# One input plane of a fused four-layer convolution: from a VectorE subtraction to a ScalarE copy and an accumulating transfer

## The chip, the cores and the metric

The kernel runs on one core of one Trainium2 chip. The metric is device time in microseconds of the whole program, as a median of several runs. Engines are named as the profile names them: PE is TensorE's matmul, PEld its weight load, DVE is VectorE, ACT is ScalarE, POOL is GpSimd, SP is SyncE, which issues most transfers.

## The reference

A batch of 128 signals with 64 channels and 1024 positions goes through four convolution layers with 3 taps each. Every layer's weights are scaled per sample by a style vector and normalised. The third layer keeps the length, the second doubles it and blurs, the fourth blurs and halves it. The input is added at the end. Cut to what matters:

```
for i, typ in enumerate(('same', 'upsample', 'same', 'downsample')):
    s = style @ mod_w[i].T + mod_b[i]
    weight = SCALE * w[i] * s[:, None, :, None]
    weight = weight * rsqrt(sum(weight * weight, axis=(2, 3)) + EPS)[:, :, None, None]
    out = conv(out, weight) + b[i]        # with a blur in 'upsample' and 'downsample'
return x + out
```

## The kernel before

No nonlinearity stands between the layers, so the kernel composes the four convolutions of each sample into one set of 9 taps (three groups of three) and applies that set to the input. The work goes in 32 quads of four samples. For one quad the taps are made in stages (scale3, stage1, stage2, stage3, combine), each a group of small matmuls on PE and a scaled copy out of PSUM on ACT. The taps are then applied by a fast-convolution scheme with five products, conv0 to conv4. Each product is a group of 24 matmul instructions over 340 columns, and each has an input tile of its own, made from the planes of X:

- X is the quad's input in SBUF, as three interleaved planes per sample pair. There are two X buffers, and SP reloads one while the other is in use.
- `T3` is plane 3 minus plane 1 and is the input of conv3. It has two buffers.
- `T12` holds the inputs of conv1 (in1) and conv2 (in2), and `T04` those of conv0 and conv4. They come from G, a combination of X planes that DVE makes (in_g01 and in_g2).

The loop is software-pipelined. Turn q computes the products of quads q and n = q+1, the taps of quad c = q+2 and the start of the chain of quad q+4. A turn's order is written out by hand in `turn_of(q)`; each engine runs its instructions in the order in which this function issues them, and semaphores do the rest. On PE a turn of the steady part is: stage2(c), conv2(q), stage3_b(c), conv4(q), stage3_a(c), conv3(n), stage1_a, conv0(q), stage1_b and share, conv1(n). On POOL it is r_sums(c) (L588), in2(n) (L731), a small sum of the S tile (L445), in1(c) (L726). On ACT stage2's copies to R are followed by the four small copies to psW that stage3_b asks for. On DVE `in3(c)` (L711) stands near the end of the turn, between sum1(n) (the tile y, L662) and the next turn's sum2 (the tile Y, L662).

Early turns (0 to 3), an entry turn (4) and the last three quads have orders of their own.

Of the kernel before, what the change touches and what calls it, by code (L numbers as in the profile page):

```python
# [49 lines left out]
AF = mybir.ActivationFunctionType  # L50
ALU = mybir.AluOpType
# [12 lines left out]
def kernel(  # L64
# [18 lines left out]
    nc_v, nc_a, nc_g = nc.vector, nc.scalar, nc.gpsimd  # L83
# [53 lines left out]
    NX = 2  # L137
    PL = NXC // 3
    Xs = [const.tile([P, 2, NXC], F32, name=f"X{i}") for i in range(NX)]

    def load(q, planes=slice(0, 3)):

        if q < NQ:
            at = slice(planes.start * PL, planes.stop * PL)
            for c in range(2):
                nc.sync.dma_start(Xs[q % NX][:, c, at], x[2 * q + c, :, at])
# [374 lines left out]
    def stage2(q, pool=None, engs=(nc_a, nc_a), between=None):  # L521
        st = chain[q]
        shared = q in shared_ps
        ps = stage2_rest(q) if shared else unit(pool or ps_w, f"psR{q}")
        for n, e in enumerate(() if shared else (-2, -1, 0, 1, 2, 3, 4, 5, 6)):
            if e % 2 == 0:
                a, lo, m = slice(1, 4), e // 2 + 1, 3
            else:
                a, lo, m = slice(4, 6), (e + 3) // 2, 2
            for r, rows in enumerate(HALF):  # L530
                for c, cols in enumerate(HALF):
                    src = st[c if r == 0 else 1 - c]
                    nc.tensor.matmul(  # L533
                        ps[r][cols, lo * C : (lo + m) * C],
                        E[rows, e + 2, :],
                        src[rows, a, :],
                        start=(n == 0),
                        stop=(n == 8),
                        skip_group_check=True,
                    )  # L540
        if between:
            between()
        t = r_pool.tile([P, 2, 9, C], F32, tag="R", name=f"R{q}")
        for r in range(2):
            scaled_copy(engs[r], flat(t[:, r, :7]), ps[r][:, : 7 * C], tC[:, q, r : r + 1])
        chain[q] = t
        return ps
# [38 lines left out]
    def r_sums(q, eng):  # L586
        t = chain[q]
        eng.tensor_add(t[:, :, 7:9], t[:, :, 2:6:3], t[:, :, 3:7:3])  # L588
# [72 lines left out]
    def sum_of(out, x, f, y, op=ALU.add):  # L661
        nc_v.scalar_tensor_tensor(out, x, f, y, op0=ALU.mult, op1=op)  # L662
# [6 lines left out]
    def combine_a(q):  # L669

        chain.pop(q)
        a, b, c, h1, h2, h3 = taps(q)
        sum_of(h1, c, -2.0, a)
        residual(q)
        sum_of(h3, h1, 1.0 / 6.0, b)

    def combine_b(q, steps=range(3)):

        a, b, c, h1, h2, h3 = taps(q)
        plan = (h2, c, -0.5, a), (h1, b, -3.0, h2, ALU.subtract), (h2, h2, -1.0 / 3.0, b)  # L680
        for i in steps:
            sum_of(*plan[i])


    NJ = NB + 2
# [7 lines left out]
    def plane(buf, i, pairs=BOTH_PAIRS):  # L693

        at = PL * (2 - i) if i < 3 else PL * 2 + 1
        return buf[:, pairs, at : at + NJ]

    def t_tile(q, tag):
        if (q, tag) not in Ts:
            Ts[q, tag] = tpool.tile([P, 2, 1 + (tag != "T3"), PL], F32, tag=tag, name=f"{tag}_{q}")  # L700
        return Ts[q, tag]

    def g_tile(q):
        if q not in Gs:
            Gs[q] = gpool.tile([P, 2, 3 * PL], F32, tag="G", name=f"G{q}")
        return Xs[q % NX], Gs[q]

    def in3(q, pairs=BOTH_PAIRS):
        if q < NQ:
            X, t = Xs[q % NX], t_tile(q, "T3")  # L710
            nc_v.tensor_sub(t[:, pairs, 0, :NJ], plane(X, 3, pairs), plane(X, 1, pairs))  # L711

    def in_g01(q, pairs=BOTH_PAIRS):
        if q < NQ:
            X, g = g_tile(q)
            sum_of(g[:, pairs, PL:], X[:, pairs, : 2 * PL], 0.5, X[:, pairs, PL:], ALU.subtract)
# [11 lines left out]
    def in2(q, eng):  # L728
        if q < NQ:
            t, g = t_tile(q, "T12"), Gs[q]  # L730
            eng.tensor_sub(t[:, :, 1, :NJ], plane(g, 2), plane(g, 1))  # L731
# [10 lines left out]
    def product(q, m, ps, groups=range(K)):  # L742

        W, H_ = Wq[q]
        tag, i = SLOT[m]
        for g in groups:
            for s, rows in enumerate(HALF):
                for c, cols in enumerate(HALF):
                    if m in (0, 4):
                        w = W[rows, tap(m // 2, g), c, :]  # L750
                    else:
                        w = H_[rows, m - 1, g, c, :]
                    nc.tensor.matmul(  # L753
                        ps[s][cols, :NB],
                        w,
                        Ts[q, tag][rows, c, i, g : g + NB],
                        start=(g == 0 and m == 3),
                        stop=(g == K - 1),
                        skip_group_check=True,
                    )  # L760
# [12 lines left out]
    def banks(q):  # L773
        return A[q] if isinstance(A[q], list) else [A[q][:, s] for s in range(2)]
# [3 lines left out]
    def open_a(q):  # L778
        A[q] = ps_conv.tile([P, 2, 512], F32, tag="u", name=f"psA{q}")
        return banks(q)  # L780

    def conv3(q, pool=None):
        if pool:
            A[q] = unit(pool, f"psA{q}")
        elif q not in A:
            open_a(q)
        product(q, 3, banks(q))
# [15 lines left out]
    def conv2(q, *groups):  # L803
        product(q, 2, banks(q), groups or range(K))

    def sum2(q, steps=(0, 1)):
        if 0 in steps:
            m3 = m3c.pop(q)
            for s, a in enumerate(banks(q)):
                sum_of(Y[:, s, :NB], m3[:, s], 3.0, a[:, :NB])  # L810
        for s, a in parts(q) if 1 in steps else ():
            nc_v.tensor_sub(y1w[q][:, s], y1w[q][:, s], a)  # L812

    def conv4(q, *groups):
        product(q, 4, Y_banks, groups or range(K))

    def conv0(q, *groups):
        product(q, 0, banks(q), groups)
# [403 lines left out]
    def high(n):  # L1222
        return Y[:, 1, NB + 4 : NB + 4 + n]
# [77 lines left out]
    def side(work, q):  # L1301
        work.get(q, lambda: None)()

    AHEAD = 3
    FIRST = AHEAD + 1

    def sharing(q):
        return FIRST < q < NQ - 4

# [104 lines left out]
    def turn_of(q):  # L1414
        n, c, s = q + 1, q + 2, q + 4
        entry = q == FIRST
        stage2(c)
        if entry:
            sum2(q)
            conv4(q)  # L1420
            combine_a(n)
            r_sums(c, nc_v)
        else:
            conv2(q)
            r_sums(c, nc_g)
            sum2(q)
            in2(n, nc_g)
        side(TABLES, q)
        for i in range(3):
            load(c + 1, slice(i, i + 1))  # L1430
        stage3_b(c, open_a(n))
        if entry:
            conv0(q, 0, 1)
        else:
            combine_a(n)
            conv4(q)
        stage3_a(c)
        combine_b(n)
        conv3(n)
        if entry:  # L1440
            copy_m3(n)
        outputs(q, 2)
        if s < NQ:
            stage1_a(s)
        if not entry:
            copy_m3(n)
        in04(n)
        if sharing(q):
            share_sums(c + 1)
        in_g2(c)  # L1450
        side(SIDE, q)
        if q in SMALL:
            l, bs = SMALL[q]
            nc_v.memset(high(bs.stop - bs.start), 0.0)
        conv0(q, *((2,) if entry else range(K)))
        if entry:
            conv1(n, 0, 1)
        outputs(q, 1)
        if s < NQ:
            stage1_b(s)  # L1460
        in_g01(c)
        if sharing(q):
            share(c + 1, banks(q))
            share_copy(c + 1)
        outputs(q, 0)
        if q in SLOTS:
            matmuls, width, rest = SLOTS[q]
            slot(matmuls, width, Y_banks)
            rest()
        if s == NQ:  # L1470
            slot(ends3, 3, unit(ps_w, "psE"), 3)
            rest3()
        if q in SMALL:
            small(q)
        conv1(n, *((2,) if entry else range(K)))
        sum1(n)
        in3(c)
        side(LATE, q)
        if s == NQ:
            in04(c)  # L1480
        in1(c, nc_g)
        if s + 1 < NQ:
            scale3(s + 1)

    for q in range(FIRST):
        early_turn(q)
    for q in range(FIRST, NQ - 3):
        turn_of(q)

    q, n, c = NQ - 3, NQ - 2, NQ - 1  # L1490
# [32 lines left out]
    q, n = NQ - 2, NQ - 1  # L1523
# [22 lines left out]
    q = NQ - 1  # L1546
# [90 lines left out]
```

## Time and profile before

| what | value |
|---|---|
| median of 3 runs | 480.38 us (480.28 to 481.21) |
| profiled execution, first to last instruction (span) | 478.0 us |
| PE busy in the span | 469.6 us |
| DVE busy | 417.5 us |
| ACT busy | 310.1 us |
| POOL busy | 163.5 us |
| bytes moved by the DMA engines | 70.70 MB |
| mean granted clock of TensorE | 0.997 |

No separate time of the profiled execution is given beside its span; the median of the runs is 2.4 us above the span, and that difference is what lies around the first and the last instruction. In a trace's list, "idle before" is how long the engine had nothing to do ahead of an instruction, and the arrow names what ended that idle time. "issue" is idle time for which the profile shows no wait at all.

### The profile page before, as it was taken

To read this page: it belongs to the slowest core of one execution; us is meant where nothing else is said; L and a number is where in the kernel's file an instruction comes from. 1 tells how busy PE (TensorE), PEld (TensorE's weight loads), DVE (VectorE), ACT (ScalarE), POOL (GpSimd) and SP (SyncE) were. 2 spreads that over 40 slices of the span, in tenths; PEclk is the share of its full clock that TensorE was granted. 3 is DMA by queue.
4 is the path that set the end of the run, shared out by engine and by line. 5 is a ranking of instruction groups with operands and counts; after the bars stand their busy time and mean duration, and the time that the engine had idled before them with its cause. 6 is when DMAs were issued, how large, how long until landed. Compare 5 with 4: busy or idle time off the path is not lost.

```text
span 478.0 us, 26721 instructions
## 1 busy us (share of the span) xinstructions
PE 469.6 (98%) x11928; PEld 346.4 (72%) x11928; DVE 417.5 (87%) x690; ACT 310.1 (65%) x708; POOL 163.5 (34%) x197
## 2 busy tenths in 40 slices
PE   8999999999999999999999999999999999999995
PEld 7877788777878876677776677766887777766652
DVE  5889998879889998899979899979989999999895
ACT  5565666667666676666667666667666768766352
POOL 3434032663335342243432233422434432333200
PEclk9999999999999999999999999999999999999998
DMA  5406365544445554345543455533455554445125
GB/s 175 158 28 200 114 195 192 150 139 144 139 150 157 173 173 127 122 151 160 171 149 120 131 170 152 173 127 126 145 169 162 162 154 146 152 146 170 61 91 191
DMA packets 50514, 70.70 MB, mean 148 GB/s; under 512 B 5664, under 2 KB 47328, under 8 KB 50400
## 3 DMA queue, kind: packets, MB, share of 16 engines
q1 hardware_dynamic: 49808, 68.32, 45.8%
q8 instruction: 93, 1.52, 1.5%
q10 hardware_dynamic: 592, 0.69, 0.5%
q14 instruction: 21, 0.17, 0.1%
HBM read 35.36 MB, written 33.62 MB: 144 GB/s over the span
## 4 chain that ended last, share of the span: by engine, by line
PE 95%; DVE 4%; issue 0%; ACT 0%; ACTq 0%; DVEq 0%
PE psA L753 45%; PE Y L753 11%; PE psR L467 9%; PE psA L571 7%; PE psW L571 7%; PE psS L389 6%; PE psR L533 4%; PE psA L467 2%; PE Y L994 2%; DVE H L662 1%; PE Y L180 1%; PE Y L336 1%; DVE G L662 0%; PE psM L204 0%; DVE o L832 0%
## 5 line engine op out<-in xcount | busy, mean ns | idle before, releaser
L753 PE MATMUL psA<-T,H 64*64 64x340 f32 x2304 | 187.3, 447 | 0.8 <-DVE y L662 0.7
L753 PEld LDWEIGHTS psA<-T,H 64*64 64x64 f32 x2304 | 89.9, 133 | 50.0 <-issue 3.1
L662 DVE SCALAR_TENSOR_TENSOR G<-X 128x1376 f32<-128x1376 f32 (+2 forms) x65 | 78.1, 1207 | 1.1 <-DMA X<-in_x 0.9
L726 POOL TENSOR_TENSOR T<-G 128x684 f32<-128x684 f32 x28 | 46.5, 1659 | 73.1 <-DVE G L662 73.1
L445 POOL TENSOR_TENSOR S<-S 128x128 f32<-128x128 f32 x28 | 22.1, 790 | 144.1 <-ACT S L360 136.8
L360 ACT ACTIVATE R<-psR,tC 128x448 f32<-128x448 f32 x63 | 36.5, 630 | 46.3 <-PE psR L467 26.7
L753 PE MATMUL psA<-T,Wf 64*64 64x340 f32 x768 | 63.9, 446 | 0.0
L753 PE MATMUL Y<-T,Wf 64*64 64x340 f32 x768 | 62.8, 451 | 0.1
L662 DVE SCALAR_TENSOR_TENSOR Y<-m,psA 128x340 f32<-128x340 f32 x64 | 33.1, 517 | 28.0 <-PE psA L753 26.6
L360 ACT ACTIVATE psW<-psA 128x128 f32<-128x128 f32 x100 | 19.3, 269 | 50.3 <-PE psA L571 46.2
L740 DVE TENSOR_TENSOR T<-G 128x1368 f32<-128x1368 f32 (+1 forms) x33 | 50.7, 1540 | 0.0
L360 ACT ACTIVATE Wf<-psW,t 128x256 f32<-128x256 f32 (+2 forms) x76 | 32.7, 479 | 26.5 <-PE psW L571 26.2
L711 DVE TENSOR_TENSOR T<-X 128x684 f32<-128x684 f32 x32 | 47.9, 1496 | 0.0
L467 PE MATMUL psR<-S,E 64*64 64x64 f32 (+1 forms) x1472 | 46.5, 238 | 0.0
L731 POOL TENSOR_TENSOR T<-G 128x684 f32<-128x684 f32 x28 | 46.5, 1660 | 0.0
L389 PEld LDWEIGHTS psS<-wd,w2n 64*64 64x64 f32 x1120 | 35.0, 133 | 13.3 <-ACT S L360 0.8
L467 PEld LDWEIGHTS psR<-S,E 64*64 64x64 f32 x1472 | 39.6, 134 | 5.2 <-ACT psR L490 0.2
L753 PEld LDWEIGHTS Y<-T,Wf 64*64 64x64 f32 x768 | 29.6, 132 | 18.0 <-DVE Y L662 0.7
L830 ACT ACTIVATE o<-psA,tb,td 128x340 f32<-128x340 f32 x63 | 37.0, 647 | 6.3 <-PE psA L753 6.3
L753 PEld LDWEIGHTS psA<-T,Wf 64*64 64x64 f32 x768 | 29.1, 133 | 15.1
L830 ACT ACTIVATE o<-Y,tb,td 128x340 f32<-128x340 f32 x63 | 36.6, 637 | 4.5 <-PE Y L753 2.7
L830 ACT ACTIVATE o<-y,tb,td 128x340 f32<-128x340 f32 x62 | 38.5, 679 | 0.6 <-DVE y L812 0.6
(165 smaller groups left out, 832.4 us busy)
## 6 DMA issues: line engine op xcount, KB each, us to landing
out<-o SPq DMA_DIRECT2D x167, 170.0 KB, 2.6
X<-in_x SPq DMA_DIRECT2D x150, 172.0 KB, 3.6
X<-in_x SPq DMA_DIRECT2D x14, 516.0 KB, 5.3
out<-o SPq DMA_DIRECT2D x6, 510.0 KB, 5.4
out<-o SPq DMA_DIRECT2D x2, 340.0 KB, 3.0
Xe<-in_x_ends SPq DMA_DIRECT2D x1, 512.0 KB, 6.7
out<-o ACTq DMA_DIRECT2D x3, 170.0 KB, 2.3
par<-in_params SPq DMA_DIRECT2D x2, 192.0 KB, 3.4
```

Of the source, the lines that this page charges most:

```text
L360: nc_a.activation(dst, src, AF.Copy, scale=f)
L389: nc.tensor.matmul(ps[r][cols, at * C : (at + n) * C], weight[rows], wd[c if r == 0 else 1 - c][rows, taps], start=first, stop=last, skip_ ...
L445: nc_g.tensor_add(t[:, :, 2], t[:, :, 2], t[:, :, 0])
L467: nc.tensor.matmul(dst[r][cols], weight[rows], st[c if r == 0 else 1 - c][rows, slots, :], start=False, stop=last, skip_group_check=True,)
L571: nc.tensor.matmul(dst[r][cols], weight[rows], t[rows, c, slots, :], start=first, stop=last, skip_group_check=True,)
L662: nc_v.scalar_tensor_tensor(out, x, f, y, op0=ALU.mult, op1=op)
L711: nc_v.tensor_sub(t[:, pairs, 0, :NJ], plane(X, 3, pairs), plane(X, 1, pairs))
L726: eng.tensor_add(t[:, :, 0, :NJ], plane(g, 2), plane(g, 1))
L731: eng.tensor_sub(t[:, :, 1, :NJ], plane(g, 2), plane(g, 1))
L740: nc_v.tensor_sub(t[:, pairs, :, :NJ], both(a, PL), both(b, 1))
L753: nc.tensor.matmul(ps[s][cols, :NB], w, Ts[q, tag][rows, c, i, g : g + NB], start=(g == 0 and m == 3), stop=(g == K - 1), skip_group_check ...
L830: nc_a.activation(dst, src, AF.Identity, bias=add, scale=d3)
```

## The change

For the quads 8 to 30 (the turns 6 to 28), T3 is made in another way. ACT writes minus plane 1 into the tile, right behind stage2's copies. A transfer that POOL issues behind in2(n) then reads plane 3 from DRAM and adds it to what stands in the tile. DVE's subtraction is dropped for these quads; for the others it stays.

```
+    def in3_negated(q):
+        X, t = Xs[q % NX], t_tile(q, "T3")
+        nc_a.activation(t[:, :, 0, :NJ], plane(X, 1), AF.Copy, scale=-1.0)
+
+    def in3_added(q):
+        t = t_tile(q, "T3")
+        at = PL * 2 + 1
+        nc_g.dma_start(
+            out=t[:, :, 0, :NJ],
+            in_=x[2 * q : 2 * q + 2, :, at : at + NJ].rearrange("b p j -> p b j"),
+            accum_op=ALU.add,
+        )
...
+    SUMMED = FIRST + 1
...
             conv2(q)
+            if q > SUMMED:
+                in3_negated(c)
             r_sums(c, nc_g)
             sum2(q)
             in2(n, nc_g)
+            if q > SUMMED:
+                in3_added(c)
...
         sum1(n)
-        in3(c)
+        if q <= SUMMED:
+            in3(c)
```

FIRST is 4. The transfer moves 128 partitions x 2 pairs x 342 numbers of 4 bytes, 342 KB, in 256 rows of 1368 bytes.

On ACT, at the start of turn 13 (c is 15), R15 are stage2's copies, psW15 those of stage3_b, Wf15 the taps. Before:

```order
L360 ACTIVATE wd17_1_4052<-w3x_141,tA_133 128x320
L360 ACTIVATE R15_4110<-psR15_0_4024,tC_136 128x448
L360 ACTIVATE R15_4110<-psR15_1_4025,tC_136 128x448
L360 ACTIVATE psW15_0_4167<-psA14_4136 128x2x64
L360 ACTIVATE psW15_1_4168<-psA14_4136 128x2x64
```

and after:

```order
L360 ACTIVATE wd17_1_4059<-w3x_141,tA_133 128x320
L360 ACTIVATE R15_4117<-psR15_0_4033,tC_136 128x448
L360 ACTIVATE R15_4117<-psR15_1_4034,tC_136 128x448
L715 ACTIVATE T3_15_4132<-X1_108 128x2x342
L360 ACTIVATE psW15_0_4177<-psA14_4146 128x2x64
L360 ACTIVATE psW15_1_4178<-psA14_4146 128x2x64
```

One instruction, L715, is put between the R copies and the psW copies.

On POOL, over the same turn, T12_14 are in1 (of the turn before) and in2 of quad 14, R15 is r_sums, S17 the small sum. Before:

```order
L726 TENSOR_TENSOR T12_14_4048<-G14_3981 128x2x342
L588 TENSOR_TENSOR R15_4110<-R15_4110 128x2x128
L731 TENSOR_TENSOR T12_14_4048<-G14_3981 128x2x342
L445 TENSOR_TENSOR S17_4243<-S17_4243 128x2x64
L726 TENSOR_TENSOR T12_15_4321<-G15_4251 128x2x342
```

and after (line numbers are 13 higher here):

```order
L739 TENSOR_TENSOR T12_14_4055<-G14_3990 128x2x342
L588 TENSOR_TENSOR R15_4117<-R15_4117 128x2x128
L744 TENSOR_TENSOR T12_14_4055<-G14_3990 128x2x342
L720 DMA T3_15_4132<-in_x 128x2x342
L445 TENSOR_TENSOR S17_4253<-S17_4253 128x2x64
L739 TENSOR_TENSOR T12_15_4329<-G15_4261 128x2x342
```

The transfer's issue, L720, stands between in2 and the small sum. It waits for ACT's L715. PE's conv3(15), in turn 14, now waits for this transfer and no longer for DVE.

## The prediction

> **What bounds the kernel now.** I read the page's busy shares first, then the chain that ended last in one steady turn, then the waits of PE in the turns that the change touches, and last the stretch of time as a whole. The page's first part and its clock row:
>
> ```profile
> PE 469.6 (98%) x11928; PEld 346.4 (72%) x11928; DVE 417.5 (87%) x690; ACT 310.1 (65%) x708; POOL 163.5 (34%) x197
> PEclk9999999999999999999999999999999999999998
> ```
>
> PE is at 98% and DVE, from which work is taken, at 87%. A share says little by itself, so here is turn 13 on the chain (start, length, what):
>
> ```profile
> 216.89 1.93 PE psR L467 x112
> 218.82 1.72 PE psA L753 x24
> 220.54 1.33 PE psA L571 x56
> 221.87 1.80 PE Y L753 x24
> 223.67 0.77 PE psW L571 x32
> 224.44 1.72 PE psA L753 x24
> ...
> 230.73 1.94 PE psR L467 x112
> ```
>
> The turn runs from 216.89 to 230.73, which is 13.84 us. Every piece of it is PE, and each starts where the one before ends. A product of 24 matmuls takes 1.72 here and in every steady turn that the chain shows. PE thus works off its instructions at one pace, with the full clock in the row above. Next, all waits of PE and of its weight loads from 116.5 to 444.8 us, which are the 23 turns 6 to 28 of the change (waiter, waited for: us in total, times, longest), and the busy times of that stretch (PE, PEld, DVE, ACT, POOL, clock, DMA share, GB/s):
>
> ```profile
> PEld Y L994 <- issue: 2.1, 10, 0.3
> PEld psA L571 <- issue: 1.7, 3, 0.8
> PE psA L571 <- issue: 0.8, 2, 0.5
> PEld psA L753 <- issue: 0.6, 3, 0.3
> PEld psA L753 <- ACT o L830: 0.3, 1, 0.3
> PEld psR L467 <- ACT psR L490: 0.2, 1, 0.2
> ```
>
> ```profile
> 116.50:444.80 328.30, 327.33 (x8894) 238.67 (x8890) 293.61 (x456) 223.47 (x523) 114.46 (x107) 1.00 0.50 151
> ```
>
> No row has DVE as what PE waited for. PE is idle for 328.30 - 327.33 = 0.97 us in 328 us, and 0.8 of it is "issue", not a wait for another engine. So these turns are bound by PE alone, and 0.97 us (0.20% of 480.38) is the most that relief of any other engine can bring. A measurement of this kernel can tell about 0.2%, 0.96 us, from no change.
>
> **The change part by part.** DVE loses 23 subtractions, and the row below prices them at 1663 ns: 38.2 us. None of it is on the chain:
>
> ```profile
> L711 DVE TENSOR_TENSOR T<-X 128x684 f32<-128x684 f32 x23 | 38.2, 1663 | 0.0
> DVE Y L662 <- PE psA L753: 23.4, 22, 1.9
> ```
>
> The next thing that DVE does after L711 is sum2 (tile Y), and it already stands idle there for PE's conv2, 23.4 us over 22 waits, about 1.1 us each. DVE will reach that wait earlier and stand there for 1.1 + 1.7 = 2.8 us. What was late is still late: PE's conv2. Gain 0. The bounds are 0 and -0.97 us.
>
> ACT gains one copy of 684 numbers in SBUF per turn. The place, and rows from which to price it:
>
> ```profile
> 218.94 1.16 ACT L360 ACTIVATE R<-psR,tC 128x448 f32<-128x448 f32 x2 [0.93 <-POOL T L726]
> 222.00 0.77 ACT L360 ACTIVATE psW<-psA 128x128 f32<-128x128 f32 x4 [1.90 <-PE psA L571]
> ACT psW L360 <- PE psA L571: 46.2, 23, 2.8
> L792 ACT COPY m<-psA 128x680 f32<-128x680 f32 x23 | 16.7, 726 | 0.0
> L830 ACT ACTIVATE o<-y,tb,td 128x340 f32<-128x340 f32 x46 | 28.7, 682 | 0.0
> ```
>
> A copy of 680 numbers out of PSUM takes 0.73 us; twice an SBUF operation of 340 would be 1.36. I take 0.9, nearer to the row of the same length. It falls into the gap between the R copies (end 218.94 + 1.16 = 220.10) and the psW copies, where ACT waits for stage3_b on PE, 46.2 us over 23 turns, 2.0 us each. Even 1.36 fits. If it did not, the psW copies would be late; they end at 222.77, and the chain's psW piece on PE starts at 223.67, which leaves another 0.9. Cost 0.
>
> POOL gains the issue of a transfer. Its turn, and the matmuls that wait for r_sums and T3:
>
> ```profile
> 220.17 0.73 POOL L588 TENSOR_TENSOR R<-R 128x256 f32<-128x256 f32 x1 [1.25 <-ACT R L360]
> 220.85 1.65 POOL L731 TENSOR_TENSOR T<-G 128x684 f32<-128x684 f32 x1
> 227.66 0.82 POOL L445 TENSOR_TENSOR S<-S 128x128 f32<-128x128 f32 x1 [5.16 <-ACT S L360]
> 231.28 1.66 POOL L726 TENSOR_TENSOR T<-G 128x684 f32<-128x684 f32 x1 [2.80 <-DVE G L662]
> 234.02 0.90 POOL L588 TENSOR_TENSOR R<-R 128x256 f32<-128x256 f32 x1 [1.08 <-ACT R L360]
> 235.31 0.40 PE L571 MATMUL psA<-R,par 64*64 64x128 f32 x8
> 238.10 1.92 PE L753 MATMUL psA<-T,H 64*64 64x340 f32 x24
> ```
>
> The issue comes at 220.85 + 1.65 = 222.50. ACT's copy is then done (about 221.0), so POOL does not stop for it. POOL has 5.16 us free before the small sum, 2.80 before in1 and 1.08 before the next r_sums: 9.0 us in all before an issue that lasts long delays r_sums. Past that, r_sums has 235.31 - 234.92 = 0.4 us to the matmul on PE that reads it. No row shows how long POOL is held by an issue. The nearest rows are SP's own issues and POOL's own operations: SP issues six loads in 2.79 us (the row below), 0.5 us each, and POOL's operation on as many numbers takes 1.65 us. I take 1 us and keep 0.5 and 3 (six of SP's issues) as ends. All of it is hidden.
>
> The transfer must land before conv3(15) at 238.10, which is 15.6 us after its issue. Rows for landing (KB each, median us to landing), for SP's part, and for the DMA engines second by second of turn 13 (share and GB/s are the last two columns):
>
> ```profile
> out<-o SPq DMA_DIRECT2D x167, 170.0 KB, 2.6
> X<-in_x SPq DMA_DIRECT2D x14, 516.0 KB, 5.3
> 219.04 2.79 SPq L146 DMA_DIRECT2D X<-in_x  x6
> 225.93 5.59 SPq L835 DMA_DIRECT2D out<-o  x6
> SPq L146 <- DVE T L711: 19.3, 16, 2.5
> 222.00:223.00 1.00, 1.00 (x20) 0.53 (x16) 1.00 (x3) 1.00 (x5) 0.51 (x1) 1.00 1.01 332
> 224.00:225.00 1.00, 1.00 (x33) 0.73 (x28) 0.93 (x2) 0.46 (x2) 0.00 (x0) 1.00 0.13 44
> ```
>
> 342 KB lies between the 170 and the 516 KB rows, 2.6 and 5.3 us; since the sum reads the tile too, I take the upper one and 8 us (half as much again) as the far end. Both are well inside 15.6, so PE does not wait: 0. The transfer meets the tail of the X loads, which fill the DMA engines up to 223 to 224 us, and the trough before the stores at 225.93. The X loads no longer wait for L711: by the last SP row they start up to 19.3/16 = 1.2 us earlier in 16 turns, and nothing waits for them that soon, since X is first read a turn later.
>
> One thing reaches PE all the same: its instructions arrive by transfers on the same engines.
>
> ```profile
> q8 instruction: 93, 1.52, 1.5%
> 122.11 0.32 PE L571 MATMUL psA<-R,par 64*64 64x128 f32 x1 [0.53 <-issue]
> 193.26 0.45 PE L571 MATMUL psA<-R,w0s 64*64 64x128 f32 x8 [0.32 <-issue]
> ```
>
> There are 93 fetches of 16 KB, and 1.5% of 16 engines over 478 us is 1.2 us each. Both gaps in which PE itself stood for "issue" fall 4 to 6 us into a turn, behind the X loads; that they are late fetches is my reading, the trace only shows the idle time. A turn moves 6 x 172 + 6 x 170 = 2052 KB beside PE, and the new transfer adds 342 KB, 17%. By bytes, 0.8 us of such gaps becomes 0.13 us more; if one more burst makes as many gaps as the loads do, it is 0.8 more. I take 0.4, between them.
>
> The Trainium skill's page "DMA: Bandwidth & Descriptors", section "Issuing engines are not separate DMA queues", says that transfers from every queue run on the same 16 DMA engines and interleave. By it a queue of its own for POOL gives the new bytes no lane of their own, which speaks for the upper end, 0.8. The sum goes by the rows.
>
> Sum: 0 (DVE) + 0 (ACT) + 0 (POOL) + 0 (landing) + 0.4 (fetches) = +0.4 us on a span of 478.0. The runs' median lies 2.4 us above that span; with the same 2.4 around it, 480.8 us.
>
> **The rivals.** *Slower by late fetches.* The mechanism above, with a larger size. Each gap costs 0.32 to 0.53 us, 0.43 on average. Three more of them (1.3 us) are enough to be slower by over 0.2%; at eight of the 23 turns it is +3.4, 483.8 us. For it speaks that the existing gaps stand behind the loads' burst; against it, that 21 turns with such a burst have no PE gap. Chance 0.21.
>
> *Slower because POOL is held.* If one issue holds POOL for more than 9.0 + 0.4 us, r_sums is late and PE's stage3_b stands. Every microsecond above that costs 23 in all: at 10 us, 0.6 x 23 = +14, 494 us. A landing over 15.6 us would cost the same way at conv3. Against it: a factor of three from the far ends that I took. Chance 0.07. The Trainium skill's page "SBUF — State Buffer", section "SBUF: two separate sides", speaks for this one: a POOL-issued transfer has its descriptors written by POOL's cores, and these are locked out while DVE runs a 2-port mode. The same page counts copies and single-input scalings among such operations and not two-input ones; DVE's rows behind 222.5 are two-input ones, so by the page no lock-out is to be expected.
>
> *Slower outside the span.* A first use of POOL as an issuer may add work before or behind the program. No row shows it; all that lies outside is 2.4 us now, and I take half as much again, +1.2 us, 481.6. Chance 0.05.
>
> *Faster.* DVE's relief would have to take away nearly all 0.97 us of PE's idle time: 479.4 us. No wait of PE on DVE supports it. Chance 0.07.
>
> **How the numbers follow.** No measurable change has 0.60, and its own range is 480.0 to 481.3. The slower rivals have 0.21 + 0.07 + 0.05 = 0.33 and the faster one 0.07. The range goes from 479.4, the bound of any gain, to 484.0, which takes in eight late fetches and leaves out the held POOL and a fetch rival that is larger still, about 1 in 10.
>
> **What would show it.** In the profile of the changed kernel: turns of 13.84 us; 23 fewer of DVE's L711; DVE's wait for PE before sum2 near 2.8 us; L715 of about 0.9 us inside a shorter wait before psW; POOL's small sum still waiting for ACT; no wait of PE for a transfer at conv3; PE's "issue" waits grown by less than 1 us. The prediction is wrong if PE waits at conv3 or at stage3_b in most turns, if "issue" gaps stand in more than three turns that had none, or if the span keeps its length and the runs do not.

## The result and the profile after

| kernel | median (lowest to highest) | runs | ratio [95% interval] |
|---|---|---|---|
| before, beside it | 480.28 us (479.77 to 481.21) | 5 | 1 |
| changed | 483.93 us (481.73 to 484.72) | 5 | 1.0073 [1.0049, 1.0096] |
| changed, on another chip (e4_again) | 481.63 us (481.27 to 483.56) | 12 | 1.0039 [1.0022, 1.0055] |

The change makes the kernel slower, by 1.9 to 3.5 us (the ratios of the two chips). The forecast was 480.8 us and no measurable change, with 479.4 to 484.0 as its range: the time lies just inside the upper end of the range, and the effect is on the side of the slower rivals. The profiled execution below is the shortest of the five, 481.73 us. Its time is 1.7 us above its span. Ratios in this document are against runs of the kernel before on the same chip. For two experiments (f2_two_sync and g3_two_pool) the comparison set some longer executions aside, so their medians lie above what their ratios give; the traces of these two are of their longest executions, 491.24 and 501.67 us.

The first parts of the page: the span, the busy shares, and the DMA queues (packets, MB, share of 16 engines).

```profile
span 480.0 us, 26752 instructions
...
PE 470.6 (98%) x11928; PEld 347.0 (72%) x11928; DVE 382.6 (80%) x667; ACT 325.5 (68%) x731; POOL 189.0 (39%) x220
...
q1 hardware_dynamic: 49808, 68.32, 45.4%
q0 software_dynamic: 6256, 8.06, 12.0%
q8 instruction: 93, 1.52, 1.4%
```

DVE went from 417.5 to 382.6 us, ACT from 310.1 to 325.5, POOL from 163.5 to 189.0. PE has the same instructions, and its share stays at 98%. q0 is the new queue: 8.06 MB took 12.0% of the DMA engines, where q1 took 45.4% for 68.32 MB. That is 1.49 against 0.66 per cent for each MB: a byte of the accumulating transfer holds an engine 2.2 times as long. Measured in engine time, the new load is 12.0/45.4 = 26% of what was there, not the 17% that its bytes make.

The chain through turn 13:

```profile
217.61 1.94 PE psR L467 x112
219.54 1.72 PE psA L766 x24
221.26 1.33 PE psA L571 x56
222.59 1.80 PE Y L766 x24
224.40 0.77 PE psW L571 x32
225.17 1.72 PE psA L766 x24
...
231.45 0.55 PE psR L467 x30
```

It runs from 217.61 to 231.45, 13.84 us, and each piece is as long as before. A steady turn has not changed. Then the waits in the 23 turns, and the busy times of that stretch (columns as in the prediction):

```profile
POOL S L445 <- ACT S L360: 84.2, 21, 4.8
...
DVE Y L662 <- PE psA L766: 57.2, 23, 2.7
...
ACT psW L360 <- PE psA L571: 30.7, 23, 2.2
...
PE psA L571 <- issue: 1.2, 2, 0.6
```

```profile
117.40:446.40 329.00, 327.79 (x8894) 238.43 (x8890) 259.66 (x434) 238.83 (x546) 139.91 (x130) 1.00 0.67 176
```

DVE now stands 57.2/23 = 2.5 us for PE's conv2 in each turn, where it stood 1.1. ACT's wait ahead of psW fell from 2.0 to 1.3 us. POOL's small sum still waits for ACT, 4.0 us each. No row has PE waiting for a transfer, for DVE or for POOL. PE's own idle time is again "issue": 1.2 us where it was 0.8. The DMA engines' share of the stretch went from 0.50 to 0.67. PE has two such gaps, as before: 0.64 us in turn 11, which had one before too, and this one in turn 20 (chain, the longest pieces):

```profile
320.57 1.94 PE psR L467 x112
322.51 1.72 PE psA L766 x24
324.23 1.32 PE psA L571 x54
325.55 0.52 issue
```

Such a gap is what late fetches of instructions would look like. This view shows no more than idle time without a wait; the packets behind it follow at the end of the experiments.

The new operations (groups by line; the DMA row has KB each and median us to landing) and one microsecond of turn 13:

```profile
L715 ACT ACTIVATE T<-X 128x684 f32<-128x684 f32 x23 | 17.8, 772 | 0.0
...
L720 POOL DMA_DIRECT2D T<-in_x x23 | 27.6, 1202 | 0.0
```

```profile
X<-in_x SPq DMA_DIRECT2D x150, 172.0 KB, 3.8
...
T<-in_x POOLq DMA_DIRECT2D x23, 342.0 KB, 5.1
```

```profile
225.00:226.00 1.00, 1.00 (x28) 0.60 (x24) 0.93 (x3) 0.74 (x3) 0.00 (x0) 1.00 0.82 75
```

In that microsecond the new transfer runs nearly alone. It fills 0.82 of the DMA engines and moves 75 GB/s; the X loads moved 332 GB/s at 1.01 in the prediction's row. The trough between loads and stores is now filled.

A single trace can't say where 2 us went. The profiled spans differ by 2.0 us, and turn 6, ahead of which nothing differs, starts at 116.57 before and at 117.46 after. Over all traces of this study that start lies between 116.57 and 119.20, and two executions of one kernel differ in it by 1.5 us (117.46 here, 118.98 in e4_again). So the causes were looked for with whole kernels and their times.

### The profile page after: what moved, and what is told of

Same layout as the page of the kernel before. It is cut to its first block, busy times and chain, and to the rows that moved or that the text cites. A ratio compares the mean times of both kernels' runs of the same rounds, so it can differ in the third digit from the quotient of the medians.

```text
span 480.0 us, 26752 instructions
## 1 busy us (share of the span) xinstructions
PE 470.6 (98%) x11928; PEld 347.0 (72%) x11928; DVE 382.6 (80%) x667; ACT 325.5 (68%) x731; POOL 189.0 (39%) x220
## 3 DMA queue, kind: packets, MB, share of 16 engines
q1 hardware_dynamic: 49808, 68.32, 45.4%
q0 software_dynamic: 6256, 8.06, 12.0%
## 4 chain that ended last, share of the span: by engine, by line
PE 94%; DVE 4%; issue 1%; ACT 0%; ACTq 0%; DVEq 0%
PE psA L766 45%; PE Y L766 11%; PE psR L467 9%; PE psA L571 7%; PE psW L571 7%; PE psS L389 6%; PE psR L533 4%; PE psA L467 2%; PE Y L1007 2%; DVE H L662 1%; PE Y L336 1%; PE Y L180 1%; DVE G L662 0%; PE psM L204 0%; DVE o L845 0%
## 5 line engine op out<-in xcount | busy, mean ns | idle before, releaser
L360 ACT ACTIVATE psW<-psA 128x128 f32<-128x128 f32 x100 | 19.3, 269 | 34.9 <-PE psA L571 30.7
L662 DVE SCALAR_TENSOR_TENSOR H<-H,Wf 128x384 f32<-128x384 f32 x64 | 35.7, 558 | 2.2
```

Source lines behind the costliest of these rows:

```text
L360: nc_a.activation(dst, src, AF.Copy, scale=f)
```

## The experiments

**First: the parts of the change.** Four kernels on one chip, 35 runs of the kernel before beside them (median 479.95 us).

*e1_no_transfer.* The changed kernel without its transfer; plane 3 is left out of T3 of quads 8 to 30.

```
-            if q > SUMMED:
-                in3_added(c)
```

> The changed kernel without its 23 transfers: ScalarE still writes the negated plane, VectorE's subtraction is still dropped, and plane 3 is left out of T3 for quads 8 to 30. Traffic theory (the transfers' bytes delay PE's instruction fetches): the whole +3.5 us goes away, 479.8 to 480.9 us. Rival, earlier X loads (they no longer wait for L711 and collide with something): still +2 to +4, 482.3 to 484.3. Rival, a fixed cost of the first use of GpSimd as an issuer: 480.3 too, so this run does not tell that one from traffic.

Measured: 480.96 us (479.68 to 484.15, 12 runs), ratio 1.0022 [1.0003, 1.0041]: +1.0 us without any new transfer.

*e2_beside.* The kernel before, and beside it the same transfer into a tile that nothing reads.

```
+    spare = const.tile([P, 2, 1, PL], F32, name="spare")
+    def beside(q):      # as in3_added, into spare
...
             in2(n, nc_g)
+            if q == SUMMED:
+                nc_g.memset(spare, 0.0)
+            if q > SUMMED:
+                beside(c)
```

> The kernel before, with VectorE's subtraction kept, and the same 23 accumulating transfers issued at the same place into a spare tile that nobody reads. Traffic theory: all of the slowdown is back without any change of the work, 482.5 to 484.7 us. If the slowdown comes from the exchange itself (PE waiting for the new T3, X loads that start earlier): 480.3 us.

Measured: 480.82 us (12 runs), ratio 1.0019 [1.0001, 1.0037]: +0.9 us from transfers on which nobody waits, far less than the 482.5 to 484.7 us that the whole slowdown would have given.

*e3_one_quad.* The change for one quad only (`q == SUMMED + 1` in place of `q > SUMMED`).

> The change for quad 8 alone, one transfer in place of 23; all other quads use VectorE. Traffic theory: 1/23 of the slowdown, 480.2 to 480.8 us. Fixed-cost theory (start, end or first use of GpSimd's queue): all of it, 482.5 to 484.7 us.

Measured: 480.15 us (12 runs), ratio 0.9998 [0.9979, 1.0017]. Nothing that a first use of POOL as an issuer costs is large enough to be seen.

*e4_again.* The changed kernel once more.

> The changed kernel once more, unaltered, for a second trace and the spread of its runs beside the kernel before on this chip. Traffic theory: 482 to 485 us, runs spread by more than 1 us, and a trace with more turns longer than 13.84 us than the first one (which was the fastest of its five runs). A fixed cost would instead put all its excess ahead of turn 6 or behind turn 28.

Measured: 1.0039, as in the table above, +1.9 us. That is about what the transfers alone (+0.9) and the rest without transfers (+1.0) give together. The three intervals overlap, so this split is not shown. Its trace does not have the longer turns that were expected: PE has one "issue" gap in the changed turns, 0.3 us.

**Second: how much traffic it takes.** Four kernels on a second chip (before: 479.8 us, 17 runs).

*f1_three_pool.* The changed kernel with two more such transfers in each turn, behind the first.

```
+    spares = [const.tile([P, 2, 1, PL], F32, name=f"spare{i}") for i in range(2)]
+    def beside(q):      # as in3_added, into each of spares
...
+            if q == SUMMED:
+                for t in spares:
+                    nc_g.memset(t, 0.0)
             if q > SUMMED:
                 in3_added(c)
+                beside(c)
```

> The changed kernel with two more accumulating transfers of the same size per turn behind its own, into two spare tiles that nobody reads: three times the added traffic and three issues of 1.2 us on GpSimd, which had 4 us left there. Traffic theory (0.9 us per 23 transfers, as the transfers beside the old kernel cost): the kernel before + 1.9 for the change + 1.8, some 483 to 484.5 us, with the excess in steps of 0.3 to 1.2 us in single turns. If the excess of the changed kernel sits in the fixed end of the program and in early X loads, the added transfers cost nothing: 481 to 482 us.

Measured: 526.19 us (524.89 to 526.53), ratio 1.096 [1.0941, 1.0979]. No theory of mine had expected +46 us. Its page's queue row, PE's waits in the changed turns, and the landing rows:

```profile
q0 software_dynamic: 18768, 24.17, 31.0%
```

```profile
PE psR L467 <- issue: 13.8, 12, 2.2
...
PE psA L571 <- issue: 11.4, 12, 2.0
...
PE psA L774 <- issue: 4.2, 4, 1.9
...
PE psA L571 <- POOL T L752: 1.3, 1, 1.3
...
PE psA L467 <- issue: 0.8, 1, 0.8
```

```profile
spare<-in_x POOLq DMA_DIRECT2D x46, 342.0 KB, 8.2
T<-in_x POOLq DMA_DIRECT2D x23, 342.0 KB, 5.2
```

30.2 us of PE's idle time are "issue" and 1.3 are a wait for POOL. The transfer that PE does need lands as fast as with one. So it isn't T3 that is late, and all but 1.3 us isn't a wait for POOL. The rest of the 46 us is in PE's busy time, 484.7 us where it was 469.6; it is looked for at the end of the experiments.

*f2_two_sync.* The kernel before, and two plain transfers of the same plane that SP issues behind the X loads of each turn.

```
+    def beside(q):      # nc.sync.dma_start into each of two spares, no accum_op
...
+        if q > SUMMED:
+            beside(c)
```

> The kernel before with two plain transfers of the same 342 KB per turn, issued by SyncE behind its X loads into spare tiles; nothing on GpSimd. If any bytes on the DMA engines delay PE's instruction fetches: before + 1.8, 481 to 483 us. If it is the GpSimd queue (its semaphores at the end of the program, its descriptors): as the kernel before, 479.5 to 480.5 us, with the end after the last matmul as short as before (5.5 us).

Measured: ratio 1.0092 [1.0062, 1.0122], +4.4 us (6 runs, 481.86 to 491.24). Twice the bytes of the change as plain transfers also cost time, and POOL has no part in it. In its trace PE has 13 "issue" gaps in the changed turns, 7.2 us in all.

*f3_old_loads.* The changed kernel with DVE's subtraction put back, into a spare tile. It has the ACT copy, the transfer and the old load on DVE, and the X loads wait for DVE's last read again.

```
         if q <= SUMMED:
             in3(c)
+        else:
+            in3_spare(c)
```

> The changed kernel with VectorE's subtraction back at its old place, but written into a spare tile, so that the X loads wait for it as in the kernel before. If the X loads that start earlier cost the 1.0 us that the kernel without transfers showed: 1.0 us less than the changed kernel, 480.5 to 481 us. If they cost nothing: as the changed kernel, 481.3 to 483 us.

Measured: 481.92 us (480.8 to 482.18), ratio 1.0040 [1.0026, 1.0054]. It is the same as the changed kernel's 1.0039. That DVE is relieved, and that the X loads start earlier for it, neither costs nor brings anything that can be seen beside the transfer.

*f4_eight_quads.* The change in turns 6 to 13 only.

> The change for the quads 8 to 15 alone, eight transfers, the other 15 of the 23 on VectorE again. Fixed-end theory (SyncE waits at the end for one semaphore more per queue slot that GpSimd's transfers used; eight transfers use all eight): the end after the last matmul is as long as with 23 transfers, 5.9 to 6.3 us against 5.5, though the last transfer is 200 us earlier. Traffic theory for the rest: a third of it. Sum: 480.4 to 481.3 us.

Measured: 480.38 us (12 runs), ratio 1.0013 [0.9999, 1.0027]. A third of the turns gives +0.6 us, which is a third of +1.9, but the interval reaches to no change. Its trace has 5.65 us from the start of the last matmul to the end, 5.54 before; the 5.9 to 6.3 that were expected did not come.

**Third: what acts without transfers, and when a transfer acts.** Four kernels on a third chip (before: 480.11 us, 23 runs).

*g1_copy_beside.* The kernel before with the ACT copy into a spare tile, in the same place.

```
             conv2(q)
+            if q > SUMMED:
+                negated_beside(c)      # as in3_negated, into spare
```

> The kernel before, with VectorE's subtraction kept, and ScalarE's copy of 684 numbers added at the change's place into a spare tile that nobody reads; no transfer. Theory: the copy lies in ScalarE's 2 us of waiting and costs nothing, 479.3 to 480.3 us, within 0.1% of the kernel before. Rival: the copy is what cost 1.0 us in the run without transfers, 480.5 to 481.5 us.

Measured: 479.95 us (12 runs), ratio 1.0003 [0.9987, 1.0018]. The copy costs nothing that can be seen.

*g2_no_transfer_again.* The same kernel as e1_no_transfer.

> The run without transfers once more, unaltered (plane 3 is left out of T3 for quads 8 to 30), for a second interval. If its +0.22% was the spread of the runs: 479.3 to 480.5 us now. If dropping VectorE's operation or adding ScalarE's really costs 1 us: 480.6 to 481.6 us again.

Measured: 481.38 us (12 runs), ratio 1.0021 [1.0004, 1.0037]. The +1.0 us came again.

*g3_two_pool.* As f1, with one more transfer and not two.

> The changed kernel with one more accumulating transfer per turn into a spare tile, two in all. With three the excess was 46 us, with one about 2. Late-fetch theory: fetches are late once the transfers are still running when the stores begin, so two lie between, by several us and clearly over twice one transfer's: 485 to 500 us, with PE's idle time put down to issue and none to a wait for a transfer. Rival, GpSimd's queue (three issues of 1.2 us late for its other work): with two issues GpSimd is in time and nothing is added, 481 to 483 us.

Measured: 488.05 to 501.67 us, ratio 1.023 [1.0184, 1.0276] from the three shorter runs, +11 us. PE's waits of its trace, in the changed turns:

```profile
PE psA L571 <- issue: 4.5, 9, 0.9
...
PE psR L467 <- issue: 4.0, 7, 1.2
...
PE psA L467 <- issue: 1.6, 3, 0.8
...
PE psA L774 <- issue: 1.6, 4, 0.5
PE psA L571 <- POOL T L752: 1.3, 1, 1.3
```

With one transfer in each turn the kernel is 2 to 4 us slower, with two 11 or more, with three 46. The cost of traffic is not in proportion to it.

*g4_late_transfer.* The changed kernel with the same one transfer issued later in the turn, behind stage1_b: in turn 13 it comes 12.8 us after the turn's start, where the changed kernel has it at 5.6.

```
             in2(n, nc_g)
-            if q > SUMMED:
-                in3_added(c)
...
+        if q > SUMMED:
+            in3_added(c)
```

> The changed kernel with the same transfers issued 5 us later in the turn, behind GpSimd's small sum of S, so that they run beside the stores and the next X loads and no longer in the trough between loads and stores. Late-fetch theory: same bytes, same instructions, but more late fetches, 483 to 490 us. Rival, a cost per transfer or per queue whatever the time of issue: as the changed kernel, 481 to 483 us. A landing too late for conv3 (4 us of slack are left) would show as PE waiting for the transfer.

Measured: 501.19 us (498.72 to 503.0), ratio 1.0442 [1.0411, 1.0472], +21 us from the place alone. First PE's waits in the changed turns, then the chain of turn 13, then four stretches of turn 14 (columns as before; a DMA share of about 1 or more means that all 16 engines are busy), then the transfer's issue, the X loads and r_sums in the timeline (start, length):

```profile
PE psA L571 <- issue: 15.2, 15, 1.8
...
PE psA L571 <- POOL T L744: 2.8, 2, 1.5
```

```profile
210.37 1.94 PE psR L467 x112
212.30 1.72 PE psA L766 x24
214.02 0.54 PE psA L571 x14
214.56 1.25 issue
215.81 1.11 PE psA L571 x33
...
225.73 0.28 PE psR L467 x12
```

```profile
227.00:228.00 1.00, 1.00 (x49) 0.97 (x45) 0.00 (x0) 0.23 (x1) 0.72 (x1) 1.00 1.12 241
228.00:229.00 1.00, 1.00 (x20) 0.90 (x15) 0.00 (x0) 1.00 (x3) 0.00 (x0) 1.00 1.16 273
229.00:230.00 1.00, 0.82 (x17) 0.55 (x11) 0.52 (x1) 0.59 (x1) 1.00 (x2) 1.00 1.04 347
230.00:231.00 1.00, 0.03 (x4) 0.04 (x4) 0.97 (x3) 0.00 (x0) 1.00 (x1) 1.00 1.10 366
```

```profile
223.13 1.19 POOL L720 DMA_DIRECT2D T<-in_x  x1
226.68 4.22 SPq L146 DMA_DIRECT2D X<-in_x  x6
229.00 0.73 POOL L588 TENSOR_TENSOR R<-R 128x256 f32<-128x256 f32 x1 [1.28 <-ACT R L360]
```

Turn 13 takes 225.73 - 210.37 = 15.36 us in place of 13.84, and 1.25 of it is one gap inside stage3_b, 4.2 us into the turn. The trace has 15 such gaps, 15.2 us in all; another 2.8 us are put down to POOL, in two waits. In turn 14 PE stands nearly all of 230 to 231, while the DMA engines are full without a break from 227 on: the transfer, issued at 223.13, runs into the X loads, issued from 226.68. The r_sums, which stage3_b reads, are done at 229.00 + 0.73 = 229.73, as early in the turn as before the change, and PE resumes only at 231: PE does not wait for them.

**What ends the gaps.** Every trace also keeps the single DMA packets. The queue q8, which brings instructions, has one packet that starts between 213.50 and 213.60 in g4's trace (row of that stretch: packets, MB, share):

```profile
q8 instruction: 1, 0.02, 56.0%
```

56% of 16 engines for 0.1 us is 0.90 us, so the packet ends near 214.4, and the gap that opened at 214.56 ends at 215.81, 1.4 us behind it. All 89 "issue" gaps of PE in the turns 6 to 28 of the 14 traces end in this way, 1.2 to 1.6 us behind the end of a packet of q8. They also stand at one place of PE's instruction list: counted over all instructions of PE and its weight loads (23986 in the kernel before), 193 or 194 places behind a multiple of 256. One packet holds about 256 of them (93 x 16384 bytes for 23986 instructions are 64 bytes each). So each gap is PE waiting for its next block of instructions.

Set beside the trace of the kernel before, matmul by matmul, f1's is 46.0 us longer from the first matmul to the last, and 40.5 of this stand at the eight places 190 to 197 of the blocks. For g3 it is 20.0 of 21.7, for g4 20.8 of 22.9 and for f2 10.2 of 11.7; this holds the longer busy time too. With one transfer in the trough no such loss shows: against the kernel before it is +0.3 us in the changed kernel's first trace, -1.1 in e4's, -1.3 in f3's and 0.0 in e2's. In g4 the 15 packets ahead of the gaps took 0.88 to 1.04 us, no longer than the mean of all 93 (1.14), so they were late because they began late. The DMA engines' share in the 2 us ahead of them was 1.11 on average, against 0.64 ahead of all fetches of the steady part. In f2 it was 0.72 against 0.66, so what holds a packet back is not shown in full.

## Why the prediction was right and where it was not

**Right, step by step.** DVE's 38.2 us were off the path. Its wait before sum2 went to 2.5 us, forecast 2.8, and f3 shows that putting the operation back changes nothing that can be seen. The copy on ACT takes 0.77 us (forecast 0.9) inside the wait ahead of psW, and costs nothing that can be seen (g1). An issue holds POOL for 1.2 us (taken 1, ends 0.5 and 3), with 4.0 us still free before the small sum; it took 1.17 to 1.36 us in each of the 23 turns, so no lock-out of POOL showed. The transfer lands in 5.1 us (taken 5.3) and PE never waits for it. SP's waits for L711 fell from 19.3 us to 1.0.

**The rivals.** *POOL held* and *landing late* are refuted by these rows. *Outside the span* is refuted too: time minus span is 1.7 us after, and 1.7 to 2.1 in every run on record, those of the kernel before among them. The 2.4 that the prediction took for before, and that stands in its forecast, compares the median of the runs with one execution's span. *Slower by late fetches* has the sign and the size of what came, but not its mechanism: it asked for such gaps in several more turns, and the traces with one transfer in the trough have two gaps (after, 1.2 us), one (e4, 0.3 us; e2, 0.6 us) and none (f3), where the kernel before has two (0.8 us). So it is luck that the time lies inside the range, 0.07 us under an upper end that was worked out from eight late fetches. Of the changed kernel only executions of 481.73 and 481.98 us were traced; what is in the longer ones, up to 484.72, is open. The mechanism itself is right where there is more traffic or where it falls on the loads: in f1, g3 and g4 PE's idle time is nearly all "issue", it grows with the number of transfers, and every gap ends behind a fetch, as shown above. f2 shows that it takes neither POOL nor an accumulating transfer. The Trainium skill's page "DMA: Bandwidth & Descriptors", section "Issuing engines are not separate DMA queues", says that all queues share the same 16 engines. The rows agree: where POOL's transfer meets SP's loads, in g4, both land later, the loads in 4.9 us (3.8 in the changed kernel) and the transfer in 6.4 (5.1):

```profile
X<-in_x SPq DMA_DIRECT2D x150, 172.0 KB, 4.9
T<-in_x POOLq DMA_DIRECT2D x23, 342.0 KB, 6.4
```

**The steps that failed.** The likeliest case, no measurable change, was wrong, because the sum had one term above zero, +0.4 us for fetches, and +1.9 to +3.5 came.

- The fetch term, +0.4, is not where the time went. PE's "issue" time in the 23 turns grew from 0.8 to 1.2 us in the first pair of traces, just as forecast, but it is 0.3 us in e4's, 0.6 in e2's and 0.0 in f3's, so the term does not stand out from what differs between executions.
- A term was missing at the end of the program, inside the span. From the start of the last product to the end of the span it takes 478.0 - 471.03 = 6.97 us before and 480.0 - 472.61 = 7.39 after (e2: 479.1 - 471.35 = 7.75):

```profile
471.03 1.90 PE L753 MATMUL psA<-T,Wf 64*64 64x340 f32 x24
```

```profile
472.61 1.90 PE L766 MATMUL psA<-T,Wf 64*64 64x340 f32 x24
```

  Over the traces, the six kernels with no or one POOL transfer have 6.7 to 7.2 us here and the eight with eight or more have 7.0 to 7.8; the means differ by 0.4 to 0.5 us. These groups touch. Counted from the landing of the last store they do not: from there to the end it takes 0.8 to 1.1 us in the six and 1.3 to 1.7 in the eight. In this stretch SP's list has 2 semaphore instructions before, 3 with one POOL transfer and 7 with eight or more, which begin 0.06 us apart: five more of them are 0.3 us. The prediction looked for what POOL's queue adds outside the span, and this stands inside it.
- A second term was missing: +1.0 us that comes without transfers (e1, g2). The copy alone does not give it (g1). What is left in those two kernels is the dropped subtraction with the earlier X loads; yet putting both back beside the transfer (f3) takes nothing away. The transfer beside the kernel (e2, 0.19%) and the copy (g1, 0.03%) make 0.22%, where f3, which has both and the subtraction, measured 0.40%; their intervals overlap, so these runs don't tell whether the missing part belongs to the dropped subtraction, to the earlier loads, or to how the parts act together. In e1's trace PE's idle time is no larger than before and its span is 477.9 us; in g2's, of the same kernel, the span is 480.6 us and 2.55 of its excess stand ahead of turn 6, where nothing differs. So no place for it was found. This stays open, and with it most of the +1.9 to +3.5.
- The fetch term was sized by bytes, 17%, and by engine time it is 26%. Here that would have moved it by tenths only. But the step also held the cost to be in proportion to the load, and g3, f1 and g4 show that it isn't: the same transfer 7 us later in the turn makes the kernel 21 us slower.

What remains between +1.9 and +3.5 us, for the same kernel on two chips, is open as well; their intervals ([1.0022, 1.0055] and [1.0049, 1.0096]) just overlap.

No version beat the kernel before. g1, e3 and f4 are equal to it within their intervals, and of the places tried for the transfer, the trough between loads and stores was the cheaper by far.

## What to carry to other kernels

When one engine is busy 98% of the span and its idle rows name no other engine, look for nothing from relieving another engine: here it brought nothing that can be seen. Price an added transfer by the time that it holds the DMA engines, not by its bytes, and look at which stretch of the loop it falls in: with the transfer in the trough this kernel was 2 to 4 us slower, with the same transfer ahead of the next burst 21. An engine that is never seen to wait for a transfer still waits for its own instructions, which come by the same DMA engines; look at the queue of the instructions when it stands idle without a wait. An effect of a few tenths of a per cent is settled by runs of kernels that differ in one part, since two traces of one kernel differ by 1.5 us before the change even begins.

## What the runs showed of the hardware that was not expected

- An accumulating transfer of 342 KB in rows of 1368 bytes holds the DMA engines 2.2 times as long for each byte as the rest of the traffic: 75 GB/s at a share of 0.82.
- PE loses time to DMA traffic whose data it does not wait for, because its own blocks of instructions come late: the kernel was 2.3% and 9.6% slower with two and three such transfers in each turn of 13.84 us, and 4.4% with one at the wrong time. PE goes on 1.2 to 1.6 us behind the end of the 16 KB packet that brings the block.
- With eight or more transfers issued by POOL the end of the program, from the last store's landing, takes 1.3 to 1.7 us in place of 0.8 to 1.1, also where nothing reads what they bring.
